# The first norm's result turned by 32x32 blocks on VectorE and by way of DRAM, with the expansion three slots later

## The chip, the cores and the metric

The kernel runs on one core of one Trainium2 chip, in one launch. The metric is the device time of that core in microseconds (us), as a median over runs. The engines are named PE (TensorE, matrix products and transposes through PSUM), DVE (VectorE), ACT (ScalarE), POOL (GpSimd) and SP (SyncE, which here only issues DMAs). PEld is the loading of weights into PE, which overlaps PE's products.

## The reference

One layer of a decoder with the norms behind the additions, in float32, for B = 16 sequences (called batches here) of T = 512 tokens with D = 256 features and 16 heads of 16:

```python
q = query @ wq + query @ Aq @ Bq * 4.0     # v likewise with Av, Bv; k = query @ wk
q, k = apply_rope(split(q)), apply_rope(split(k))
scores = where(causal, -1e9, q @ k.T / sqrt(16))
x = layernorm(x + softmax(scores) @ v @ wo)            # the first norm
h = butterfly(x @ W_exp + b_exp, up_weights, 1024)     # ten stages of 2x2 mixings
h = gelu(h + up_bias, approximate=False)
y = butterfly(h, down_weights, 1024) @ W_con + b_con + down_bias
out = layernorm(x + y)                                 # the second norm
```

## The kernel before

**Folded weights.** The ten butterfly stages are linear, so they are multiplied into the weights once: `wup` (256 x 1024) for the way up and `wdn` (1024 x 256) for the way down. This work is cut into tasks (`fold_tasks`) that a table `tasks_at` spreads over the first slots, up to slot 44. What is left of the second half for each batch is: `hidden` (the expansion: `ph` = `wup` times the turned x1, in 8 chunks of 128 units, L633), `gelus` (ACT), and `contract` (`py` = h times `wdn`, four token tiles t, each in two halves of four chunks, L660).

**Slots.** The order of all work is written out by hand: every engine runs its instructions in the order of the program. The program is a list of slots. A batch has four quads (two halves c of the heads, and an even and an odd head, par), each of five slots, so 20 slots (`per`). Slot s does `largest` for one block of scores of batch s/20 (PE L421, DVE L430 takes the row maxima) and `weights` for the same block of 15 slots before (PE L479 computes the scores again, with the row maximum taken off; ACT L493 takes the exponential, POOL L497 clears what lies above the diagonal). `weigh` (L521) multiplies the weights with v. A slot has a kind u = s mod 5; u = 0 and 1 work on 512 and u = 2 and 3 on 384 + 128 columns, u = 4 on 256 from both pairs. The two score tiles `pa` and `pb` have a single buffer each: the next slot's scores can be written when DVE and ACT have read these.

**Everything else** is hung onto slots: `add(s, f)` puts f behind the slot's scores and its `weigh`; `holes` come behind those. Within a slot the calls stand in the order in which they were added, batch by batch. For a batch that begins at slot s:

- `project_v` (pvv, L383) for the four token tiles, at s-3, s-1, s+4, s+14; `project` (pqk, L337, with a DVE copy L344 or L348, and the swap DMAs L351) for batch b+1 in the order of `chains`, all four in the hole of slot s+10; `turn` and `part` (POOL, ACT and a row of ones by DMA, L372) follow.
- `load_x` (the residual into z, L94) at s+9; `place_largest` (the maxima turned and written into a row of q by way of DRAM, L448 to L457) at s+11 and s+21.
- `normalize` (L553 reciprocal of the sums, L554 multiply), for c = 0 at s+27, 28, 29, 31 and for c = 1 at s+36, 37, 39, 40.
- `project_out` (L559; DVE adds the residual in L567 and takes statistics in L577 and L578) at s+41 and s+42, `spread`, `offset` and `centre` (L589 to L602, the first norm) at s+42, 43, 44.
- `turn_x1` at s+45: eight PE transposes (L616) into two of the three banks of `ps_w`, two DVE copies (L617) into `x1T`, and an addition of the biases to z on POOL (L621).
- `hidden` in pairs of chunks at s+46 to s+49 (DVE L644 or ACT L646 copy `ph` out, for chunks 0 and 4 and for the others), the eight `gelus` in the hole of s+50.
- `contract` halves at s+51, 52, 53, 55, 56, 58, 60, 63, each tile with the DVE chain L668, L577, L578; `spread` at s+63, `offset` at s+67, `centre` and `store` (L672) at s+68.

The last two batches have no later one to hide in; their second halves follow at the end with lists of their own. `largest` ends at slot 319, and the slots behind hold `weights` alone.

Of the kernel before, what the change touches and what calls it, by code (L numbers as in the profile page):

```python
# [11 lines left out]
F32 = mybir.dt.float32  # L12
BF16 = mybir.dt.bfloat16
AF = mybir.ActivationFunctionType
ALU = mybir.AluOpType
PSUM = bass.MemoryType.PSUM

P = 128
NH = 16
DH = 16  # L20
HG = 32
NG = P // HG
# [11 lines left out]
def decoder_layer(  # L34
# [18 lines left out]
    nc = tc.nc  # L53
    B, T, D = x.shape
    NT = T // P
    NC = D // P
    DHID = wcon.shape[0]
    NHC = DHID // P
# [5 lines left out]
    ring2 = ctx.enter_context(tc.tile_pool(name="ring2", bufs=2))  # L64
# [3 lines left out]
    dram = ctx.enter_context(tc.tile_pool(name="dram", bufs=4, space=bass.MemoryType.DRAM))  # L68
# [5 lines left out]
    def bank(name, shape):  # L74
        return ps_w.tile(shape, F32, tag="w", name=name)
# [10 lines left out]
    xTs, zs = {}, {}  # L86
# [24 lines left out]
    bias2 = const.tile([P, 2, D], F32, name="bias2")  # L111
# [197 lines left out]
    def fold_tasks():  # L309
        def up():  # L310
            yield from all_across(0, ya, DA)
            yield idle, lambda: nc.vector.tensor_add(
                hbias, ya[:, :, D : D + 1].rearrange("p c o -> p (c o)"), ubias
            )
            yield idle, lambda: nc.vector.tensor_add(
                bias2[:, 0, :], bias2[:, 0, :], bias2[:, 1, :]
            )

        def down():
            yield from all_across(1, wdn, D)  # L320
            yield from all_within(1, wdn, D)


        last = [
            (idle, lambda d=d, half=half: up_done(d, half))
            for d in range(NC)
            for half in range(2)
        ]
        return list(all_within(0, ya, DA)), mixed(down(), up()) + last
# [130 lines left out]
    state = {}  # L460
# [86 lines left out]
            nc.sync.dma_start(rows_of(sums, 1), rows_of(x, 0))  # L547
            nc.sync.dma_start(rows_of(even, 1), rows_of(x, 1))

    def normalize(b, c, t):  # L550
        x, sums = state["heads", b, c]
        ts = slice(t * P, (t + 1) * P)
        nc.vector.reciprocal(sums[:, ts], sums[:, ts])  # L553
        nc.vector.tensor_tensor(x[:, ts], x[:, ts], sums[:, ts], ALU.mult)  # L554

    def project_out(b, t):
        pw = bank(f"pwo_{b}_{t}", [P, D])
        for c in range(NC):
            nc.tensor.matmul(  # L559
                pw,  # L560
                state["heads", b, c][0][:, t * P : (t + 1) * P],
                wo_sb[:, c, :],
                start=(c == 0),
                stop=(c == NC - 1),
            )
        z = zs[b]
        nc.vector.tensor_add(z[:, t, :], pw, z[:, t, :])  # L567
        stats_of(1, b, t)
# [23 lines left out]
    def offset(which, b, t0=0, t1=NT):  # L592
        stats, norm = state["stats", which, b], state["norm", which, b]
        ts = slice(t0, t1)
        nc.vector.scalar_tensor_tensor(  # L595
            norm[:, 2, ts], stats[:, ts, 0], -1.0, norm[:, 1, ts], ALU.mult, ALU.mult
        )
# [10 lines left out]
            )  # L608


    def turn_x1(b, c):
        if c == 0:
            state["x1T", b] = ring2.tile([P, NC, T], F32, tag="x1T", name=f"x1T_{b}", bufs=1)
        pt = bank(f"pt1_{b}_{c}", [P, NT, P])
        for t in range(NT):
            nc.tensor.transpose(pt[:, t, :], zs[b][:, t, c * P : (c + 1) * P], ident)  # L616
        nc.vector.tensor_copy(  # L617
            state["x1T", b][:, c, :], pt.rearrange("p t q -> p (t q)")
        )
        if c == NC - 1:  # L620
            nc.gpsimd.tensor_tensor(  # L621
                zs[b],
                zs[b],
                bias2[:, 0:1, :].to_broadcast([P, NT, D]),
                ALU.add,
            )

    def hidden(b, hc, fused=False):
        if hc == 0:
            state["h", b] = hpool.tile([P, NHC, T], F32, tag="h", name=f"h_{b}")  # L630
        ph = bank(f"ph_{b}_{hc}", [P, T])
        for c in range(NC):
            nc.tensor.matmul(  # L633
                ph,
                wup[:, c, hc * P : (hc + 1) * P],
                state["x1T", b][:, c, :],
                start=(c == 0),
                stop=(c == NC - 1),
            )
        h = state["h", b][:, hc, :]  # L640
        if fused:
            nc.scalar.activation(h, ph, AF.Gelu, bias=hbias[:, hc : hc + 1])
        elif hc % 4 == 0:
            nc.vector.tensor_copy(h, ph)  # L644
        else:
            nc.scalar.copy(h, ph)  # L646

    def gelus(b, count=NHC):
        h = state["h", b]
        for hc in range(count):  # L650
            nc.scalar.activation(
                h[:, hc, :], h[:, hc, :], AF.Gelu, bias=hbias[:, hc : hc + 1]
            )
# [31 lines left out]
    per = PER_QUAD * NQ  # L685
    behind = PER_QUAD * BEHIND
# [3 lines left out]
    others = {s: [] for s in range(-head, last)}  # L690
    holes = {}
    chains = [(c, side) for c in range(NC) for side in range(2)]

    def add(s, f, *args):
        others[s].append(lambda: f(*args))

    def start_projection(b, side, c):
        state["pr", b, side, c] = project(b, side, c)
# [13 lines left out]
    for b in range(B):  # L712
        s = b * per
        if b > 0:

            at = {1: (-16, -11, -13, -9), B - 1: (-1, 4, 10, 10)}.get(b, (-3, -1, 4, 14))
            for t in range(NT):
                add(s + at[t], project_v, b, t)
        if b + 1 < B:

            add(s - head * (b == 0), load_xT, b + 1)
            at = {0: (2, 5, 7, 10), 1: (3, 6, 8, 11)}.get(b, (10, 10, 10, 10))
            for i, (c, side) in enumerate(chains):
                holes.setdefault(s + at[i], []).append(
                    lambda b=b, side=side, c=c: start_projection(b + 1, side, c)
                )
                turning = s + max(at[0] + 1 + 3 * i, at[i] + 1)
                for step in range(3):
                    add(turning + step, turn, b + 1, side, c, step)
                for step in range(1 + side):  # L730
                    add(turning + (6 if i == 3 else 4) + step, part, b + 1, side, c, step)
        add(s + 9, load_x, b)
        add(s + 11, place_largest, b, 0)
        add(s + 21, place_largest, b, 1)
        for c in range(NC if b + 1 < B else 1):
            for t in range(NT):
                at = (27, 28, 29, 31) if c == 0 else (36, 37, 39, 40)
                add(s + (at[t] if b + 1 < B else 29 + t), normalize, b, c, t)
        if b + 1 < B:
            for t in range(NT):  # L740
                add(s + 41 + t // 2, project_out, b, t)
            add(s + 42, spread, 1, b)
            add(s + 43, offset, 1, b)
            add(s + 44, centre, 1, b)
            for c in range(NC):
                add(s + 45 + (b + 2 == B), turn_x1, b, c)
        if b + 2 < B:

            late = 2 * (b + 3 == B)
            for hc in range(NHC - late):  # L750
                add(s + 46 + hc // 2, hidden, b, hc)
            holes.setdefault(s + 50, []).insert(0, lambda b=b, late=late: gelus(b, NHC - late))
            for hc in range(NHC - late, NHC):
                holes[s + 50].append(lambda b=b, hc=hc: hidden(b, hc, True))
            for t in range(NT):
                for half in range(2):
                    at = (11, 12, 13, 15, 16, 18, 20, 23)[2 * t + half]
                    if b + 3 == B and t == NT - 1:
                        at = (23, 25)[half]
                    add(s + 40 + at, contract, b, t, half)  # L760
            add(s + 63 + 2 * (b + 3 == B), spread, 2, b)
            add(s + 67, offset, 2, b)
            add(s + 68, centre, 2, b)
            add(s + 68, store, b)

# [2 lines left out]
    for hc, at in enumerate((7, 8, 9)):  # L770
        add(edge + at, hidden, y, hc)
# [8 lines left out]
    for t in range(NT):  # L780
        add(end + 2, normalize, z, NC - 1, t)
# [10 lines left out]
    for c in range(NC):  # L792
        add(end + 5, turn_x1, z, c)
# [13 lines left out]
    first, second = fold_tasks()  # L807
    fold = first + second
    tasks_at = dict(zip(range(2, behind), (0, 1, 2, 3, 4, 4, 5, 5, 5, 6, 9, 11, 14)))
    for s in range(behind, 2 * per + 5):  # L810
        tasks_at[s] = len(first) + -(-len(second) * (s - behind + 1) // (2 * per + 5 - behind))
    ahead = 0
    given = 0
    due = deque()
# [12 lines left out]
    for s in range(-head, last):  # L827
# [7 lines left out]
        if kinds and not (len(kinds) == 1 and kinds[0][2] % 2):  # L835
# [7 lines left out]
            elif u == PER_QUAD - 1:  # L843


                blocks = [(2, r, ps) for r, ps in enumerate((pair0, pair1))]
# [3 lines left out]
            else:  # L850
                for i, (fn, quad, _) in enumerate(kinds):
                    blocks = [(k, (r + i) % 2) for k, r in SLOTS[u]]
# [135 lines left out]
```

## Time and profile before

| | before |
|---|---|
| median of 3 runs | 1364.14 us (1358.62 to 1364.54) |
| the profiled execution | 1357.15 us |
| its span | 1355.4 us, granted PE clock 0.993 of full speed |
| PE busy | 1320.3 us (97%), 8728 instructions |
| DVE busy | 925.8 us (68%) |
| ACT busy | 707.3 us (52%) |
| POOL busy | 510.9 us (38%) |
| row maxima (L430, 384 columns) | 878 of 499 ns |
| expansion products (L633) | 512 of 604 ns, 235.8 us busy |
| contraction products (L660) | 1024 of 391 ns, 252.1 us busy |

The page of the profile gives the busy time of each engine, the chain of work that ended last with its shares by engine and line, and groups of instructions by line: busy us, mean ns of one, idle time before them and what ended it. Matmuls are pipelined: the length of a record is its latency, so what a row of them costs PE is read from the start of the first to the start of the next group in the timeline. Timeline rows give the start in us, the length, the engine, the line, what was written and read, shapes, and how many were joined in the row.

### The profile page before, as it was taken

The numbers are of one execution on the slowest core, as the hardware profiler recorded it, in microseconds if no ns is written. First come the engines' busy times: TensorE is split into PE (matmuls) and PEld (weight loads), VectorE is DVE, ScalarE is ACT, GpSimd is POOL, SyncE is SP. The second block draws the span as 40 slices with busy tenths as digits, with TensorE's granted clock in tenths as the row PEclk, the third lists the DMA queues.
The fourth block names the chain that finished last, engine by engine and source line by source line (L and its number), as shares of the span: only waits on it lengthen the run. The fifth ranks groups of instructions, "written<-read, shape, count | busy, mean of one in ns | idle before, by whom it ended". The sixth has DMA issues, their size and how long they took to land.

```text
span 1355.4 us, 23859 instructions
## 1 busy us (share of the span) xinstructions
PE 1320.3 (97%) x8728; PEld 702.5 (52%) x8728; DVE 925.8 (68%) x2949; ACT 707.3 (52%) x1079; POOL 510.9 (38%) x777
## 2 busy tenths in 40 slices
PE   8898999999999999999999999999999999998998
PEld 4453545455454545555454554545555454554555
DVE  4788757667685766758577685857768685776632
ACT  2575454454646445464645545464554546445643
POOL 3534215344251533425153352515335252531311
PEclk9998999999999999999999999999999999999999
DMA  5311010110102011010110101010110101000000
GB/s 172 120 45 45 22 59 30 40 45 30 68 30 74 30 41 45 30 67 30 67 35 31 57 30 68 30 60 30 40 60 30 68 30 55 30 27 32 30 12 31
DMA packets 45685, 63.49 MB, mean 47 GB/s; under 512 B 5752, under 2 KB 26232, under 8 KB 45568
## 3 DMA queue, kind: packets, MB, share of 16 engines
q1 hardware_dynamic: 41680, 56.42, 11.8%
q10 hardware_dynamic: 3888, 5.55, 1.3%
q8 instruction: 69, 1.13, 0.3%
q14 instruction: 48, 0.39, 0.1%
HBM read 23.40 MB, written 8.91 MB: 24 GB/s over the span
## 4 chain that ended last, share of the span: by engine, by line
PE 84%; DVE 11%; ACT 3%; issue 2%; DMA 0%; POOLq 0%; POOL 0%; DVEq 0%; SPq 0%; ACTq 0%
PE pb L479 19%; PE ph L633 17%; PE py L660 16%; PE po L521 10%; PE pqk L337 8%; DVE junk L430 5%; PE pvv L383 4%; PE pwo L559 3%; PE pa L421 3%; DVE bn L577 1%; PE pb L421 1%; PE pt L616 1%; ACT pT L493 1%; PE pa L479 1%; DVE z L567 1%
## 5 line engine op out<-in xcount | busy, mean ns | idle before, releaser
L430 DVE CUSTOM_DVE_ANT_0 junk<-pa,causal 128x384 bf16<-128x384 f32 (+2 forms) x878 | 438.3, 499 | 235.0 <-PE pa L421 176.1
L493 ACT ACTIVATE pT<-pb 128x1024 f32<-128x1024 f32 (+1 forms) x314 | 293.8, 936 | 377.3 <-PE pa L421 227.6
L497 POOL TENSOR_SCALAR_AFFINE_SELECT pT<-pT 128x256 f32<-128x256 f32 x512 | 202.5, 407 | 733.3 <-ACT pT L493 731.6
L479 PE MATMUL pb<-qz,kz 17*128 17x512 f32 (+2 forms) x1756 | 328.8, 473 | 16.1 <-ACT pT L493 12.1
L421 PE MATMUL pa<-kz,qz 32*128 32x384 f32 (+3 forms) x1756 | 329.2, 474 | 4.2 <-DVE mx L430 4.2
L660 PE MATMUL py<-wdn,h 128*128 128x256 f32 x1024 | 252.1, 391 | 0.0
L479 PEld LDWEIGHTS pb<-qz,kz 17*128 17x128 f32 (+1 forms) x1756 | 142.9, 183 | 179.5 <-issue 82.2
L633 PE MATMUL ph<-x1T,yb 128*128 128x512 f32 x512 | 235.8, 604 | 0.0
L660 PEld LDWEIGHTS py<-wdn,h 128*128 128x128 f32 x1024 | 185.1, 189 | 72.2 <-issue 36.2
L521 PE MATMUL po<-pT,vaug 128*32 128x512 f32 (+3 forms) x2048 | 179.5, 446 | 0.0
L633 PEld LDWEIGHTS ph<-x1T,yb 128*128 128x128 f32 x512 | 92.4, 189 | 122.3 <-issue 97.6
L421 PEld LDWEIGHTS pa<-kz,qz 32*128 32x128 f32 (+1 forms) x1756 | 143.7, 184 | 13.6 <-DVE mx L430 11.2
L553 DVE RECIPROCAL sums<-sums 128x128 f32<-128x128 f32 x128 | 121.1, 946 | 0.0
L337 PE MATMUL pqk<-xT,wqk 128*128 128x512 f32 x256 | 118.5, 613 | 0.0
L646 ACT COPY h<-ph 128x512 f32<-128x512 f32 x84 | 49.2, 585 | 123.2 <-PE ph L633 123.2
L521 PEld LDWEIGHTS po<-pT,vaug 128*32 128x32 f32 x2048 | 47.1, 109 | 102.3 <-issue 78.2
L430 DVE DVE_READ_ACCUMULATOR2_ANT mx<- 128x1 f32 x1024 | 84.5, 82 | 0.0
L337 PEld LDWEIGHTS pqk<-xT,wqk 128*128 128x128 f32 x256 | 48.0, 194 | 61.9 <-issue 57.4
L365 POOL TENSOR_TENSOR swap<-swap,rope_sb 128x512 f32<-128x512 f32 x62 | 79.6, 1283 | 0.0
L602 ACT ACTIVATE z<-z,norm 128x256 f32<-128x256 f32 x128 | 66.7, 589 | 24.6 <-DVE norm L595 24.5
L668 DVE TENSOR_TENSOR z<-py,z 128x256 f32<-128x256 f32 x64 | 27.1, 423 | 74.1 <-PE py L660 73.9
L430 DVE CUSTOM_DVE_ANT_0 junk<-pb,causal 128x256 bf16<-128x256 f32 (+3 forms) x146 | 63.6, 436 | 17.3 <-PE pa L421 4.0
(91 smaller groups left out, 1334.2 us busy)
## 6 DMA issues: line engine op xcount, KB each, us to landing
xT<-in_xT SPq DMA_DIRECT2D x16, 512.0 KB
swap<-qz SPq DMA_DIRECT2D x64, 128.0 KB
swap<-kz SPq DMA_DIRECT2D x64, 128.0 KB
z<-in_x SPq DMA_DIRECT2D x16, 512.0 KB
sums<-x SPq DMA_DIRECT2D x64, 128.0 KB
out_y<-z SPq DMA_DIRECT2D x15, 512.0 KB
x<-x SPq DMA_DIRECT2D x32, 128.0 KB
early<-in_wexpT ACTq DMA_DIRECT2D x1, 1028.0 KB
```

Of the source, the lines that this page charges most:

```text
L337: nc.tensor.matmul(pq, wqk[:, d, e : e + P], xTs[b][:, d, :], start=(d == 0), stop=(d == NC - 1))
L365: engine.tensor_tensor(swap, swap, rope_sb[:, 1, :], ALU.mult)
L421: lambda i=i, rows=rows, at=at, n=n, t=t, ps=ps: nc.tensor.matmul(ps[:, i, at : at + n], q[rows, par, t * P : n], k_[rows, par, 0:n], star ...
L430: lambda i=i, at=at, n=n, t=t, g=g, ps=ps: nc.vector.tensor_tensor_reduce(out=junk[:, 0:n], in0=ps[:, i, at : at + n], in1=causal[:, T - n ...
L479: lambda i=i, rows=rows, at=at, n=n, k=block, ps=ps: nc.tensor.matmul(ps[:, i, at : at + n], kt[rows, par, k * P : (k + 1) * P], qt[rows, ...
L493: nc.scalar.activation(pT[:, heads, 0:n], ps[:, :, at : at + n], AF.Exp)
L497: nc.gpsimd.affine_select(out=diag, in_=diag, pattern=[[0, 2], [1, P]], compare_op=ALU.is_ge, fill=0.0, base=0, channel_multiplier=-1,)
L521: nc.tensor.matmul(po[HG * g : HG * (g + 1), k * P : T], vaugs[b % 2][:, k, NG * c + g, first : first + HG], pT[:, g, at : at + n], start= ...
L553: nc.vector.reciprocal(sums[:, ts], sums[:, ts])
L602: nc.scalar.activation(zs[b][:, t, :], zs[b][:, t, :], AF.Identity, bias=norm[:, 2, t : t + 1], scale=norm[:, 1, t : t + 1],)
L633: nc.tensor.matmul(ph, wup[:, c, hc * P : (hc + 1) * P], state["x1T", b][:, c, :], start=(c == 0), stop=(c == NC - 1),)
L660: nc.tensor.matmul(py, state["h", b][:, hc, t * P : (t + 1) * P], wdn[:, hc, :], start=(hc == 0), stop=(hc == NHC - 1),)
```

## The change

For batches 0 to 13, the PE transposes and the two copies out of PSUM are replaced. DVE transposes each token tile of z in 32x32 blocks (four instructions of 128 x 256, SBUF to SBUF); four DMAs on SP, one for each band of 32 partitions, place the blocks in a DRAM tile, 128 KB each; and one DMA reads the tile back as `x1T` (512 KB), with tokens in blocked order. `hidden` reads it by a pattern with runs of 32. Batches 14 and 15 keep the transposes on PE. Around it the order of the slots is changed: the transposes stand ahead of slot s+45's other calls, the addition of the biases comes at s+47, the expansion begins at s+49 instead of s+46, with its last chunk fused with its gelu, and the contraction, the second norm and the store follow later. `project` is no longer all in one hole: one at s+7 and three at s+13. `project_v` moves by one to three slots, `load_x` by eleven, `normalize` is split into `invert` and `scale`, and the fold tasks are spread up to slot 47.

```diff
-    def normalize(b, c, t):
+    def invert(b, c, t):
+        sums = state["heads", b, c][1]
+        ts = slice(t * P, (t + 1) * P)
+        nc.vector.reciprocal(sums[:, ts], sums[:, ts])
+
+    def scale(b, c, t):
         x, sums = state["heads", b, c]
         ts = slice(t * P, (t + 1) * P)
-        nc.vector.reciprocal(sums[:, ts], sums[:, ts])
         nc.vector.tensor_tensor(x[:, ts], x[:, ts], sums[:, ts], ALU.mult)
...
+    def turn_x1_by_blocks(b):
+        blocks = ring2.tile([P, D // HG, NT, HG], F32, tag="blocks", name=f"blocks_{b}", bufs=1)
+        for t in range(NT):
+            nc.vector.transpose(blocks[:, :, t, :], zs[b][:, t, :])
+        turned = dram.tile([D // HG, HG, NG, P], F32, tag="turned", name=f"turned_{b}")
+        for n in range(NG):
+            nc.sync.dma_start(
+                turned[:, :, n, :].rearrange("f j k -> j f k"),
+                blocks[HG * n : HG * (n + 1)].rearrange("j f t i -> j f (t i)"),
+            )
+        x1T = ring2.tile([P, NC, T], F32, tag="x1T", name=f"x1T_{b}", bufs=1)
+        nc.sync.dma_start(x1T, turned.rearrange("(c f) j n k -> (f j) c (n k)", c=NC))
+        state["x1T", b] = x1T.rearrange("p c (n t i) -> p c t n i", t=NT, i=HG)
...
-                state["x1T", b][:, c, :],
+                state["x1T", b][:, c],
...
-            at = {1: (-16, -11, -13, -9), B - 1: (-1, 4, 10, 10)}.get(b, (-3, -1, 4, 14))
+            at = {1: (-16, -11, -13, -9), B - 1: (13, 13, 13, 13)}.get(b, (-3, 0, 5, 15))
...
-            at = {0: (2, 5, 7, 10), 1: (3, 6, 8, 11)}.get(b, (10, 10, 10, 10))
+            at = {0: (2, 5, 7, 10), 1: (3, 6, 8, 11)}.get(b, (7, 13, 13, 13))
...
-        add(s + 9, load_x, b)
+        add(s + 20, load_x, b)
...
-                at = (27, 28, 29, 31) if c == 0 else (36, 37, 39, 40)
-                add(s + (at[t] if b + 1 < B else 29 + t), normalize, b, c, t)
+                if b + 1 == B:
+                    add(s + 29 + t, normalize, b, c, t)
+                    continue
+                add(s + ((29, 30, 31, 32), (37, 38, 39, 40))[c][t], invert, b, c, t)
+                add(s + ((29, 30, 31, 32), (37, 38, 40, 41))[c][t], scale, b, c, t)
...
-            add(s + 43, offset, 1, b)
+            others[s + 43].insert(0, lambda b=b: offset(1, b))
             add(s + 44, centre, 1, b)
+        if b + 2 == B:
             for c in range(NC):
-                add(s + 45 + (b + 2 == B), turn_x1, b, c)
+                add(s + 46, turn_x1, b, c)
         if b + 2 < B:
-            late = 2 * (b + 3 == B)
-            for hc in range(NHC - late):
-                add(s + 46 + hc // 2, hidden, b, hc)
-            holes.setdefault(s + 50, []).insert(0, lambda b=b, late=late: gelus(b, NHC - late))
...
+            others[s + 45].insert(0, lambda b=b: turn_x1_by_blocks(b))
+            add(s + 47, add_biases, b)
+            for hc in range(NHC - 1):
+                add(s + 49 + (hc + 1) // 2, hidden, b, hc)
+            holes.setdefault(s + 53, []).insert(0, lambda b=b: gelus(b, NHC - 1))
+            holes[s + 53].append(lambda b=b: hidden(b, NHC - 1, True))
+            at = (14, 16, 18, 19, 23, 24, 26, 28)
+            if b + 3 == B:
+                at = (14, 16, 18, 19, 20, 23, 24, 25)
             for t in range(NT):
                 for half in range(2):
-                    at = (11, 12, 13, 15, 16, 18, 20, 23)[2 * t + half]
...
+                    add(s + 40 + at[2 * t + half], contract, b, t, half)
+            add(s + 40 + at[-1], spread, 2, b)
+            add(s + 70, offset, 2, b)
+            add(s + 71, centre, 2, b)
+            add(s + 72, store, b)
...
-    for s in range(behind, 2 * per + 5):
+    for s in range(behind, 2 * per + 8):
```

## The prediction

> **What bounds the kernel now.** I read three views in this order: busy time of each engine, then one batch of the steady part, then single slots of that batch. Page parts 1 and 4:
>
> ```profile
> PE 1320.3 (97%) x8728; PEld 702.5 (52%) x8728; DVE 925.8 (68%) x2949; ACT 707.3 (52%) x1079; POOL 510.9 (38%) x777
> PE 84%; DVE 11%; ACT 3%; issue 2%; DMA 0%; POOLq 0%; POOL 0%; DVEq 0%; SPq 0%; ACTq 0%
> ```
>
> PE is nearly always busy, but 11% of the chain that ends last is DVE. The busy times of stretches cut at the first transpose (L616) of successive batches show that the middle repeats:
>
> ```profile
> 645.40:725.10 79.70, 79.51 (x541) 42.10 (x540) 56.12 (x183) 42.64 (x63) 31.66 (x47) 1.00 0.13 45
> 725.10:804.80 79.70, 79.52 (x542) 42.09 (x541) 56.16 (x181) 42.63 (x63) 31.68 (x47) 1.00 0.13 45
> ```
>
> The columns are length, PE, PEld, DVE, ACT and POOL busy, granted clock, DMA share, GB/s. A batch takes 79.7 us and PE is busy in 79.5 of them, at a granted clock of 1.00. So any PE work that goes is time that goes, unless PE then waits. Whether it waits is seen in single slots. PE's timeline around 762 us (start, length, instruction):
>
> ```profile
> 762.39 0.59 PE L479 MATMUL pb<-qz,kz 32*128 32x384 f32 x2
> 763.47 1.99 PE L660 MATMUL py<-wdn,h 128*128 128x256 f32 x8
> 765.40 0.48 PE L479 MATMUL pb<-qz,kz 32*128 32x256 f32 x2
> 765.53 0.48 PE L421 MATMUL pa<-kz,qz 16*128 16x256 f32 x2
> ```
>
> and DVE's:
>
> ```profile
> 763.63 0.56 DVE L430 CUSTOM_DVE_ANT_0 junk<-pa,causal 128x384 bf16<-128x384 f32 x1
> ...
> 765.39 0.08 DVE L430 DVE_READ_ACCUMULATOR2_ANT mx<- 128x1 f32 x1
> 766.71 0.42 DVE L430 CUSTOM_DVE_ANT_0 junk<-pa,causal 128x256 bf16<-128x256 f32 x1 [1.24 <-PE pa L479]
> ```
>
> The slot starts at 762.39. DVE takes up its row maxima 1.24 us later and is done at 765.47; the next slot's scores (L421), which write the same PSUM, begin 0.06 us after that, 0.11 us later than they could. That gives the rule I use: **a slot lasts as long as its PE work, or until its row maxima end plus 0.06 us, whichever is longer.** Maxima take 1.42 us in slots of kind 0 and 1, 1.84 in kinds 2 and 3, 1.94 in kind 4 (slot number mod 5). Undisturbed they ask for 2.7, 3.1 and 3.2 us. If DVE is held by earlier work the maxima begin late, and the lateness falls on PE. At 795.89 two chains of L567, L577 and L578 held them until 797.34 instead of 797.13; they ended at 799.16, and the scores due at 798.91 came at 799.22: 0.31 us lost. Such losses add up to 1.3 us a batch before (slots 13 to 15, 18 to 20 and 23 to 25, counted from a batch's first).
>
> **What goes.** Per batch, for 14 of 16 batches, eight transposes and two copies. The groups of the two lines (busy us, mean ns, idle before):
>
> ```profile
> L616 PE MATMUL pt<-ident,z 128*128 128x128 f32 x128 | 17.6, 280 | 0.0
> L617 DVE COPY x1T<-pt 128x512 f32<-128x512 f32 x32 | 20.5, 683 | 0.0
> ```
>
> and PE's timeline at one batch's eight:
>
> ```profile
> 804.28 1.09 PE L616 MATMUL pt<-ident,z 128*128 128x128 f32 x8
> 805.30 0.70 PE L479 MATMUL pb<-qz,kz 17*128 17x512 f32 x2
> ```
>
> The 280 ns are latency; eight take 804.28 to 805.30 = 1.02 us of PE, and 14 x 1.02 = **14.3 us** go. Two copies of 0.683 us on DVE go as well.
>
> **What comes on DVE.** Four block transposes 128x256 f32, SBUF to SBUF, none in this trace. The nearest rows: batch statistics read the same 128x256 from SBUF in 0.428 us (L577); a 128x128 multiply takes 0.29 at least, 0.98 at most when it meets POOL (L554); a 128x128 reciprocal 0.947 (L553). Bounds 0.30 and 0.95, value 0.43, because L577 has the same size and place: 1.7 us for four. They stand ahead of the slot-45 work, wait for ACT's centre (L602), and in my count end about 1.6 us into slot 46, whose maxima then come late by 0.3: PE loses 0.07 us there. At 0.30 it loses nothing; at 0.62, 0.83; at 0.95, 2.15 us a batch.
>
> [...]
>
> **What comes on the queues.** SP gets four issues of 128 KB into DRAM, then a read of 512 KB that waits for them. A single issue takes 0.33 to 0.56 us on SP (rows 0.33, ones row 0.56), so four are 2 us; a small write (rows<-mT) to the read behind it takes 758.78 to 760.25 = 1.5 us; the 512 KB store to the load that waits for it takes 740.36 to 743.82 = 3.5 us. Chain about 2 + 2 + 3.5 = 7.5 us after the transposes end. The first expansion product now comes at slot 49, about 12 us after slot 46 starts, 10 after they end: hidden with some 2.5 us to spare. Behind the waiting read on SP stand the ones row (L372), the next swaps (L351) and the sums (L544); from their places they are due after the read can go. ACT and POOL get no new work. Cost 0. The DMA share in the steady part is 0.13, so bandwidth is free; bounds 0 and, at twice the chain, 15 us, 5 us a batch.
>
> L633 reads x1T in runs of 32 elements instead of 512. No row shows such a read by PE. Nearest is ACT's write of vaug in strides of two (L391: 256 elements in 0.39 us; 512 contiguous ones, L646, in 0.585), no dearer for it. The other bound: a product cut into four of 128 columns would go at the transposes' 0.127 each, 0.508 instead of 0.454 us (3.63 us for the eight of two chunks), 12% of 14.5 us a batch (4 x 3.63) = 1.7. Value 0.
>
> **What moves.** The PE work of a steady batch falls from 78.06 to 77.03 us. With the rule above, slot by slot, losses are 2.2 us instead of 1.3 (1.09 and 2.29 in my count). Two places make it:
> - Slot 59 (39 of the next batch) is of kind 4 and now ends with the second half of contract t=1. DVE, in program order, waits for that product, adds and takes statistics (0.42 + 0.43 + 0.18, about 1.05 with gaps), and then inverts t=2 of the next batch (0.95) ahead of the maxima of slot 60. These begin 2.1 us into it rather than 1.24, end at 3.56, and the slot holds only 2.67 us of PE work (scores, po and a pvv that moved in): **0.95 us lost a batch**. Before, slot 59 held only the pair L553/L554, and slot 60 had 3.57 us of PE work to cover it.
> - Slot 63: scale t=2, inverse and scale t=3 of c=1 now stand in slots 60 and 61, ahead of four L567 chains (1.05 each); the maxima of 63 begin 1.95 us into it instead of 1.24: 0.85 lost in 63, 0.45 before.
> The other edges are as before within 0.1. Of the projections three share one hole; the one that reuses a bank waits for a copy of 0.69 us while 1.77 us of another product runs. Cost 0.
>
> **Sum.** PE work -14.3. Steady losses 12 batches x (2.29 - 1.09) = +14.4, partly what I round to 1.0 from the trace's own 1.3 before: +11 to +14, I take 12. Start (slots 16 to 50): fold work spread to slot 47 with short slots between, losses 29.1 against 22.5 in the same count: +6.5, though before's real start has some 7 us more waits (on ACT) than I can count, so 0 to +6.5, I take 4. End: slots 300, 305, 307, 315 become too short (2.0 + 1.1 + 1.1 + 1.1), 303, 314, 319 no longer are (3.3): +1.9; two contract halves more (3.84 us) run beside waits of the last slots: -1.1. Sum -14.3 + 12 + 4 + 1.9 - 1.1 = **+2.5 us**. The profiled execution took 1357.15 us (1.75 around its span), 7 below the median 1364.14 of runs from 1358.62 to 1364.54. 1357 + 2.5 = 1360; from the median, 1367. I say 1363.
>
> **Rivals.**
> - *The losses are covered* (chance 0.27). If DVE's slack takes up the new chains, as it would if the slot-59 inverse ran before the add in time or ACT's side of the start shrinks, only PE's -14.3 and part of the end stays: 1345 to 1352. For it: PE 97% busy. Against: the 0.31 us at 798.9, from a smaller jam.
> - *The blocks are dear* (0.17). One mechanism: four transposes in slots 45 and 46 delay the maxima of 46. It decides from 0.43 us apiece; at 0.62 it gives 12 x 0.8 = +9 on top (1373), at 0.95 +25 (1388). For it: L554's 0.98 beside POOL, L553's 0.95. Against: L577.
> - *The new x1T is slow* (0.14): read in runs, 1.7 us x 14 = +24 (1387); or late from DRAM, +5 x 13 = +65 at twice the chain, and less from 10 us on. Nothing speaks for it but the absence of a row.
> - *Nothing to gain, transposes free already*: excluded by 804.28 to 805.30, PE dense on both sides.
>
> **Numbers.** Forecast 0.42, rivals 0.27, 0.17, 0.14. The measurement can't tell less than 0.5% (6.8 us: 1357.3 to 1371.0) from no change. Faster 0.27, same 0.42, slower 0.31. The forecast's own range is 1357 to 1370. The 8-in-10 range leaves out the lowest faster cases and the dearest slow ones: 1345 to 1386.
>
> **What would show it.** Right: steady batch 79.3 to 79.7 us; slot 60's scores of the next slot wait some 0.9 us for L430; transposes near 0.43 us; first L633 of a batch waiting for nothing. Wrong: a batch of 78.5 us or less (losses covered); transposes above 0.6 us with PE waiting at slot 46 to 47; L633 above 592 ns, or waiting for the read of x1T.

## The result, and the profile after

The changed kernel takes 1365.06 us (median of 20 runs, 1359.01 to 1370.56) against 1361.04 us for the kernel before (20 runs): a ratio of 1.0035 with a 95% interval of 1.0022 to 1.0049. That is slower by 0.35%: inside the predicted range and within the 0.5% that the prediction called "same", but clear of noise. The 1363 on record lay 1 us below the median of 1364.14 that was shown for before, so it forecast a slight gain, and the kernel became slightly slower. Run once more beside the experiments it gave 1.0042 (1.0026 to 1.0058). Two runs of all that follow (3682 us in the sixth experiment, 1407 us in the eighth) stood far apart from the others of their kernels and are left out of the medians.

The profiled execution after took 1363.26 us, with a span of 1361.5 us and a mean granted clock of 0.984 (0.993 before). Busy times, and the chain that ended last:

```profile
PE 1324.7 (97%) x8616; PEld 694.3 (51%) x8616; DVE 915.9 (67%) x2977; ACT 700.9 (51%) x1067; POOL 511.7 (38%) x777
PE 80%; DVE 14%; ACT 3%; issue 2%; DMA 0%; POOLq 0%; POOL 0%; DVEq 0%; ACTq 0%
```

112 transposes are gone and PE is still busy 97% of a longer span; in the chain PE's share fell from 84% to 80% and DVE's rose from 11% to 14%. Two steady batches of the changed kernel, cut at the first block transpose of each (columns as in the prediction):

```profile
567.96:647.47 79.51, 79.10 (x531) 41.18 (x530) 55.50 (x183) 41.90 (x62) 31.65 (x48) 1.00 0.19 58
647.47:726.98 79.51, 79.11 (x532) 41.13 (x530) 55.59 (x183) 41.96 (x62) 31.71 (x48) 1.00 0.19 58
```

A batch takes 79.5 us, as before. (Before it was 79.54, not 79.70: the prediction cut its stretches 0.16 us too long. The two rows of transposes at 724.74 and 804.28 give 79.54.) So **1.02 us of PE work a batch went and nothing was gained**. Where it went is seen at slots 59 to 61 (slot 59 starts at 542.78). DVE, then PE:

```profile
547.02 0.42 DVE L695 TENSOR_TENSOR z<-py,z 128x256 f32<-128x256 f32 x1 [0.96 <-PE py L687]
547.48 0.43 DVE L585 BATCH_NORM_STATS2 bn<-z 128x6 f32<-128x256 f32 x1
547.94 0.18 DVE L586 BATCH_NORM_AGGREGATE stats<-bn 128x2 f32<-128x6 f32 x1
548.04 0.92 DVE L553 RECIPROCAL sums<-sums 128x128 f32<-128x128 f32 x1
548.88 0.63 DVE L430 CUSTOM_DVE_ANT_0 junk<-pa,causal 128x512 bf16<-128x512 f32 x1
550.17 0.87 DVE L558 TENSOR_TENSOR x<-x,sums 128x128 f32<-128x128 f32 x1
```

```profile
546.91 0.70 PE L479 MATMUL pb<-qz,kz 32*128 32x512 f32 x2
548.55 1.13 PE L383 MATMUL pvv<-wv_sb,xT 128*128 128x256 f32 x4
549.62 1.13 PE L479 MATMUL pb<-qz,kz 32*128 32x512 f32 x4
550.30 1.13 PE L421 MATMUL pa<-kz,qz 16*128 16x512 f32 x4
```

DVE idles 0.96 us for the contraction, adds, takes statistics, inverts, and only then, 1.97 us into slot 60, begins the row maxima (L430). These end at 550.25; the scores of slot 61 (L421), which stand 0.02 us behind the slot's start when nothing holds them, come at 550.30 instead of 549.64: some 0.67 us lost. The loss doesn't look like a wait, because PE's records leave no gap in slot 61 up to the next product at 551.36:

```profile
549.62:551.36 1.74, 1.74 (x9) 0.59 (x8) 1.74 (x4) 1.01 (x3) 1.27 (x2) 1.00 0.23 75
```

The four score products of L479 run first and alone, and the four of L421 then take 550.30 to 551.36 = 1.06 us. Undisturbed, the two kinds run side by side and all eight take about that long (the first experiment shows it). So the share of busy time hides this loss, and a slot's length shows it. The blocks themselves, on DVE and then on SP:

```profile
567.96 1.42 DVE L644 STREAM_TRANSPOSE blocks<-z 128x256 f32<-128x256 f32 x4
569.31 0.69 DVE L430 CUSTOM_DVE_ANT_0 junk<-pa,causal 128x512 bf16<-128x512 f32 x1
```

```profile
569.41 2.05 SPq L647 DMA_DIRECT2D turned<-blocks  x4
573.62 0.38 SPq L652 DMA_DIRECT2D x1T<-turned  x1
```

Four transposes take 1.42 us in all, end 1.3 us into slot 46 (568.08), and its maxima begin at 569.31, on time. Issue and landing of the writes take 4.2 us; the read starts at 573.62 and the expansion at 580.26 waits for nothing.

By place, from the starts of slots in the timelines of the two profiled executions, the 6.1 us between the spans are (work that moved from one place to another included): up to slot 60 +0.8 us, slots 60 to 300 -0.2, slots 300 to 319 -0.1, from slot 319 to the end +5.6.

### The profile page after: what moved, and what is told of

It reads as the page before. It is cut to its first block, busy times and chain, and to the rows that moved or that the text cites. A ratio compares the mean times of both kernels' runs of the same rounds, so it can differ in the third digit from the quotient of the medians.

```text
span 1361.5 us, 23681 instructions
## 1 busy us (share of the span) xinstructions
PE 1324.7 (97%) x8616; PEld 694.3 (51%) x8616; DVE 915.9 (67%) x2977; ACT 700.9 (51%) x1067; POOL 511.7 (38%) x777
## 4 chain that ended last, share of the span: by engine, by line
PE 80%; DVE 14%; ACT 3%; issue 2%; DMA 0%; POOLq 0%; POOL 0%; DVEq 0%; ACTq 0%
PE pb L479 17%; PE ph L660 17%; PE py L687 16%; PE po L521 10%; PE pqk L337 8%; DVE junk L430 6%; PE pa L421 3%; PE pvv L383 3%; DVE bn L585 2%; DVE sums L553 2%; PE pb L421 1%; ACT pT L493 1%; DVE z L575 1%; PE pa L479 1%; PE pwo L567 1%
## 5 line engine op out<-in xcount | busy, mean ns | idle before, releaser
L430 DVE CUSTOM_DVE_ANT_0 junk<-pa,causal 128x384 bf16<-128x384 f32 (+2 forms) x878 | 436.2, 497 | 184.6 <-PE pa L421 143.1
L479 PE MATMUL pb<-qz,kz 17*128 17x512 f32 (+2 forms) x1756 | 333.3, 479 | 18.1 <-ACT pT L493 12.5
L421 PE MATMUL pa<-kz,qz 32*128 32x384 f32 (+3 forms) x1756 | 334.1, 480 | 4.6 <-DVE mx L430 4.6
L479 PEld LDWEIGHTS pb<-qz,kz 17*128 17x128 f32 (+1 forms) x1756 | 143.6, 185 | 189.2 <-issue 83.4
L660 PE MATMUL ph<-x1T,yb 128*128 128x512 f32 x512 | 239.6, 607 | 0.0
L421 PEld LDWEIGHTS pa<-kz,qz 32*128 32x128 f32 (+1 forms) x1756 | 144.5, 186 | 24.7 <-DVE mx L430 22.6
L660 PEld LDWEIGHTS ph<-x1T,yb 128*128 128x128 f32 x512 | 91.2, 189 | 121.6 <-issue 114.1
L337 PE MATMUL pqk<-xT,wqk 128*128 128x512 f32 x256 | 122.3, 620 | 0.0
L430 DVE CUSTOM_DVE_ANT_0 junk<-pb,causal 128x256 bf16<-128x256 f32 (+3 forms) x146 | 63.6, 436 | 33.4 <-ACT pT L493 17.5
L430 DVE DVE_READ_ACCUMULATOR2_ANT mx<- 128x1 f32 x1024 | 84.3, 82 | 0.0
L673 ACT COPY h<-ph 128x512 f32<-128x512 f32 x72 | 41.9, 581 | 75.5 <-PE ph L660 75.5
```

What stands on the lines that cost most here:

```text
L337: nc.tensor.matmul(pq, wqk[:, d, e : e + P], xTs[b][:, d, :], start=(d == 0), stop=(d == NC - 1))
L421: lambda i=i, rows=rows, at=at, n=n, t=t, ps=ps: nc.tensor.matmul(ps[:, i, at : at + n], q[rows, par, t * P : n], k_[rows, par, 0:n], star ...
L430: lambda i=i, at=at, n=n, t=t, g=g, ps=ps: nc.vector.tensor_tensor_reduce(out=junk[:, 0:n], in0=ps[:, i, at : at + n], in1=causal[:, T - n ...
L479: lambda i=i, rows=rows, at=at, n=n, k=block, ps=ps: nc.tensor.matmul(ps[:, i, at : at + n], kt[rows, par, k * P : (k + 1) * P], qt[rows, ...
L660: nc.tensor.matmul(ph, wup[:, c, hc * P : (hc + 1) * P], state["x1T", b][:, c], start=(c == 0), stop=(c == NC - 1),)
```

## The experiments

All are compared with the kernel before, run beside them on the same chip (medians 1359.9 us for the first four, 1358.8 for the fifth to eighth and 1360.2 for the others).

**1. The reciprocal first.** In slot 59:

```diff
-                add(s + ((29, 30, 31, 32), (37, 38, 39, 40))[c][t], invert, b, c, t)
+                at = s + ((29, 30, 31, 32), (37, 38, 39, 40))[c][t]
+                others[at].insert(0 if (c, t) == (1, 2) else len(others[at]), lambda b=b, c=c, t=t: invert(b, c, t))
```

> The changed kernel with one edit: in slot 59 the reciprocal of c=1, t=2 stands ahead of the addition of the contraction tile instead of behind it; nothing is left out. Theory (DVE's order gives the gain back): the row maxima of slot 60 then begin 1.2 to 1.3 us into the slot instead of 2.0, the scores of slot 61 wait no longer, and a steady batch falls from 79.50 to 78.6-78.8 us; over 13 to 14 batches 10 to 12 us less than the changed kernel, some 1353-1355 us beside a kernel before of 1361. Rival (what was lost lies in the start and at the end, and the DVE jam is covered by something else that would wait next): no more than 2 us gained.

Measured: 1348.97 us, ratio 0.992 (0.9893 to 0.9947), 16 us below the changed kernel, where 10 to 12 were expected. DVE at slots 59 and 60 (slot 60 starts at 542.39):

```profile
541.45 0.95 DVE L553 RECIPROCAL sums<-sums 128x128 f32<-128x128 f32 x1
542.50 0.42 DVE L695 TENSOR_TENSOR z<-py,z 128x256 f32<-128x256 f32 x1
542.96 0.43 DVE L585 BATCH_NORM_STATS2 bn<-z 128x6 f32<-128x256 f32 x1
543.42 0.18 DVE L586 BATCH_NORM_AGGREGATE stats<-bn 128x2 f32<-128x6 f32 x1
543.63 0.69 DVE L430 CUSTOM_DVE_ANT_0 junk<-pa,causal 128x512 bf16<-128x512 f32 x1
```

The reciprocal now fills the time in which DVE waited for the product, and the maxima begin 1.24 us into slot 60. In slot 61 the two kinds of score products start side by side again, and all eight are through at 546.17, 1.08 us after the first:

```profile
545.09 0.70 PE L479 MATMUL pb<-qz,kz 32*128 32x512 f32 x2
545.12 0.70 PE L421 MATMUL pa<-kz,qz 16*128 16x512 f32 x2
```

A steady batch takes 78.31 us:

```profile
558.31:636.62 78.31, 78.16 (x532) 40.73 (x531) 55.01 (x184) 41.96 (x63) 31.84 (x47) 1.00 0.19 59
```

Of the 1.2 us a batch, slot 61 gives 0.67 (3.78 to 3.11 us) and slot 64 gives 0.48 (4.94 to 4.46), where part of the lateness had been handed on to. So the loss of the steady part was this order, not the blocks.

**2. The transposes back on PE,** at the new places of all else:

```diff
-        if b + 2 == B:
+        if b + 1 < B:
             for c in range(NC):
-                add(s + 46, turn_x1, b, c)
+                add(s + 45 + (b + 2 == B), turn_x1, b, c)
...
-            others[s + 45].insert(0, lambda b=b: turn_x1_by_blocks(b))
-            add(s + 47, add_biases, b)
```

> The changed kernel with the transposes back on PE at slot s+45 (turn_x1 for all batches, no DRAM tile), all else at its new place; the same result. Theory (the blocks save 1.02 us of PE a batch and cost next to nothing themselves; the new order costs the rest): a steady batch of 80.4-80.5 us, 13 to 14 us more than the changed kernel, some 1378 us. Rival (the block transposes, their DMAs or the read of x1T in runs cost time of their own): less than 8 us more than the changed kernel.

Measured: 1375.61 us, ratio 1.0103 (1.0076 to 1.013), some 10 us above the changed kernel, between what theory (13 to 14) and rival (under 8) had named; the batch 80.32 us. So in the new order the blocks save 0.8 us a batch, 11 in all: slot 45 grew from 2.70 to 3.53 us only. There the eight transposes and the four products of pvv behind them take 1.89 us together (646.87 to 648.76), 0.82 more than the 1.07 of the products alone, where the transposes took 1.02 us in the kernel before. And the new order alone costs 80.32 - 79.54 = 0.8 us a batch. The two cancel.

**3. The fold as before.**

```diff
-    for s in range(behind, 2 * per + 8):
+    for s in range(behind, 2 * per + 5):
```

(and the same 5 in the divisor below it).

> The changed kernel with the fold tasks spread up to slot 44 as before instead of 47; the same result. Theory (the start loses by the granted clock and by waits, not by where the fold ends): within 2 us of the changed kernel, with the granted clock again 0.98-0.99 on the mean. Rival (the longer fold makes short slots 43 to 48 in which PE waits and its clock falls): 3 to 6 us less than the changed kernel and a mean clock nearer 0.99.

Measured: 1366.23 us, ratio 1.0048 (1.0032 to 1.0063), clock 0.9865 in the median. The longer fold is not what costs.

**4. The blocks alone,** in the kernel before, with the expansion left at s+46:

```diff
-            for c in range(NC):
-                add(s + 45 + (b + 2 == B), turn_x1, b, c)
+            if b + 2 < B:
+                others[s + 45].insert(0, lambda b=b: turn_x1_by_blocks(b))
+                add(s + 47, add_biases, b)
+            else:
+                for c in range(NC):
+                    add(s + 46, turn_x1, b, c)
```

> The kernel before with the block transposes and the way through DRAM in place of the transposes on PE, the biases added at s+47, and the expansion left at s+46; the same result. It prices the chain that the three slots hide. Theory: x1T is there 7.5 to 8 us after the transposes end, these end 1.3 us into slot 46, the expansion could begin 1.1 us into it, so PE waits 7.5 to 8.5 us in each of 13 to 14 batches: 90 to 110 us more than before. Rival (the read lands much sooner, the three slots were not needed): under 40 us more.

Measured: 1506.55 us (two runs), ratio 1.1071 (1.1031 to 1.111): 147 us more. The wait is the one foretold; PE's waits (us in all, times, longest):

```profile
PE ph L657 <- DMA x1T<-turned: 116.1, 14, 8.7
```

From the end of the transposes (712.8) to the first product (721.0) it is 8.2 us. What had not been foretold is the clock. Two-microsecond stretches (PE busy is the second number, the clock the third from the end):

```profile
712.00:714.00 2.00, 0.61 (x8) 0.00 (x0) 1.97 (x6) 1.02 (x1) 0.34 (x1) 0.83 0.35 128
718.00:720.00 2.00, 0.00 (x0) 0.00 (x0) 0.00 (x0) 0.00 (x0) 0.00 (x0) 0.50 0.81 181
722.00:724.00 2.00, 2.00 (x4) 0.94 (x3) 0.00 (x0) 0.00 (x0) 0.00 (x0) 0.50 0.00 0
726.00:728.00 2.00, 2.00 (x7) 0.65 (x9) 0.00 (x0) 0.31 (x1) 0.00 (x0) 0.76 0.00 0
```

Here PE works at half clock for 6 us after the wait is over (721.0 to 727.0), which costs about another 3 us, the half of it. The steady batches take 89.7 to 91.3 us, 90.4 on the mean. This, and that the runs' times went with their mean clocks, made the clock the next question.

**5. The order put further right:** on top of the first experiment,

```diff
-                add(s + ((29, 30, 31, 32), (37, 38, 40, 41))[c][t], scale, b, c, t)
+                add(at, scale, b, c, t)
...
-                add(s + 41 + t // 2, project_out, b, t)
-            add(s + 42, spread, 1, b)
-            others[s + 43].insert(0, lambda b=b: offset(1, b))
+                add(s + (41, 41, 42, 43)[t], project_out, b, t)
+            add(s + 43, spread, 1, b)
+            others[s + 44].insert(0, lambda b=b: offset(1, b))
```

> The changed kernel with the reciprocal of c=1, t=2 ahead of the contraction's addition as in the first experiment, the multiplications of t=2 and t=3 one slot earlier, and the output projection's last tile with its spread and offset one slot later, so that DVE's four chains stand in three slots; nothing is left out. Theory (DVE's order in slots 59 to 64 sets what is left of the waits): the steady batch falls from 78.3 us in the first experiment by 0.1 to 0.4 us, 1 to 5 us less in all, some 1345-1348. Rival (what is left are waits of slot edges that no order takes away): within 1 us of the first experiment.

Measured: 1346.18 us, ratio 0.9908 (0.9889 to 0.9928), the batch 78.13 us, 0.18 below the first experiment, in the low part of the 0.1 to 0.4 that were expected. It beats both kernels.

**6, 7 and 8. Idle products in three slots,** in the changed kernel, in the fifth experiment and in the kernel before:

```diff
+        if s in (32, 33, 34):
+            pf = bank(f"fill_{s}", [P, T])
+            for _ in range(2):
+                nc.tensor.matmul(pf, wo_sb[:, 0, 0:P], rope_sb[:, 0, :], start=True, stop=True)
```

> The changed kernel with idle work added: two products of 128x128 by 128x512 into a PSUM bank that nobody reads, behind the other work of each of slots 32, 33 and 34 (about 5.4 us of PE in all), where PE waits for DVE and ACT near 118 to 128 us and the granted clock then stands at 0.5 until 138 us. Theory (those waits lower the clock, and the lower clock costs the time by which the changed kernel is slower): the half-clock stretch from 121 to 138 us goes or shrinks, the mean clock rises by 0.003 to 0.006, and the kernel is 2 to 7 us faster than the changed one although PE does more. Rival (the clock follows something else, or costs nothing): the clock stays and the kernel is 0 to 5 us slower.

> The new order of the fifth experiment and the idle products of the sixth together; nothing is left out. If both theories hold the gains add: 2 to 7 us less than the fifth experiment, about 1340-1345. If the clock is not what the idle products move: 0 to 5 us more than the fifth.

> The kernel before with the same idle products in the same three slots, whose own trace has a half clock from 121 to 130 and 136 to 140 us. Theory (the clock's loss in the start has nothing to do with the change): 2 to 6 us less than before and a mean clock up by 0.003 to 0.005. Rival: 0 to 5 us more.

Measured: 1362.12 us, 1.0028 (1.0013 to 1.0042); 1341.91 us, 0.9885 (0.9865 to 0.9905); 1359.55 us, 1.0009 (0.9993 to 1.0024). The place where the clock fell did change. The changed kernel, then the same with idle products:

```profile
120.00:124.00 4.00, 3.06 (x24) 1.87 (x26) 3.86 (x14) 1.82 (x3) 1.69 (x4) 0.65 0.20 74
124.00:128.00 4.00, 3.57 (x28) 1.52 (x28) 3.79 (x10) 1.19 (x2) 2.35 (x4) 0.50 0.00 0
132.00:136.00 4.00, 4.00 (x16) 1.69 (x12) 2.52 (x6) 2.96 (x6) 0.85 (x2) 0.50 0.18 66
```

```profile
121.00:125.00 4.00, 3.66 (x30) 1.52 (x28) 3.79 (x12) 1.20 (x2) 2.00 (x4) 1.00 0.00 0
125.00:129.00 4.00, 3.52 (x27) 1.29 (x21) 3.71 (x7) 2.42 (x4) 3.70 (x3) 1.00 0.09 33
137.00:141.00 4.00, 3.66 (x29) 1.72 (x30) 3.29 (x13) 1.73 (x3) 0.81 (x2) 0.61 0.00 0
```

The half clock from 121 to 138 us is gone, but it comes back at 138 behind the next waits. Mean clocks rose (medians 0.9845 to 0.991; 0.985 to 0.992; 0.990 to 0.991), the times fell less: by the ratios to before about 1 us in the sixth, where 2 to 7 were expected, 4 in the seventh, as expected, and none in the eighth, where 2 to 6 were. In the sixth the idle products may have taken most of what the clock gave; no run here separates the two.

**9 and 10. Idle products in eleven slots** (17, 19, 25, 29, 32 to 34, 38, 39, 44, 49; one or two each), in the changed kernel and in the fifth experiment, and **the changed kernel again**:

> The changed kernel with idle products of the same kind in eleven slots of the start that end in a wait of PE (17, 19, 25, 29, 32 to 34, 38, 39, 44, 49; about 13 us of PE), nobody reads them. Theory (waits of about 1 us and more in the start are what drops the clock): hardly any half-clock stretch is left between 55 and 200 us, the mean clock is 0.993 or more, and the kernel is 2 to 6 us faster than the changed one in the same call, since most of the idle products stand where PE waits. Rival (the idle products only take the place of what the clock cost): the time of the changed kernel or up to 5 us more.

> The order of the fifth experiment with the idle products in eleven slots: the candidate for the best version. Theory: 0 to 4 us less than order and idle products in three slots (a ratio to before of 0.985 to 0.989). Rival: the additional idle products cost more than the clock gives, ratio 0.990 or more.

> The changed kernel itself once more, beside the others of this call on one chip, so that its clock and time and those of the kernel before are compared there. Theory (its steady part equals the kernel before, and what it loses it loses by the granted clock in the start): 3 to 5 us above before, the mean clock 0.002 to 0.004 lower, and at one clock the two agree within 1 us. Rival (the difference is waits, whatever the clock): at one clock still 3 us or more apart.

Measured: 1363.44 us, 1.0024 (1.0014 to 1.0034); 1345.43 us, 0.9885 (0.9867 to 0.9903); 1366.75 us, 1.0042 (1.0026 to 1.0058). By the ratios the ninth lies about 2.5 us below the changed kernel run beside it, inside the 2 to 6 expected, with a clock of 0.992 against 0.985; the tenth is no better than the seventh. These runs don't show how much the clock costs, since each mends it by adding work.

**11. The block transposes twice.**

```diff
-            nc.vector.transpose(blocks[:, :, t, :], zs[b][:, t, :])
+            for _ in range(2):
+                nc.vector.transpose(blocks[:, :, t, :], zs[b][:, t, :])
```

> The changed kernel with each of the four block transposes done twice over (same output). It tests the step on slot 46. Theory (the row maxima of slot 46 begin when the transposes end, and PE has 0.07 us or less to spare there): four take 1.42 us, eight 2.8 us; slot 46 lengthens by 1.1 to 1.3 us in each of 13 to 14 batches, 15 to 18 us more than the changed kernel. Rival (DVE's lateness is absorbed by the slots after): under 5 us more.

Measured: 1399.23 us, ratio 1.0277 (1.0252 to 1.0302): 32 us above the changed kernel, twice what was expected. Eight took 3.34 us rather than 2.8 (one of them 0.444 us in the median, where it was 0.403 in the changed kernel; why isn't shown), so the maxima of slot 46 were 1.9 us late, and a batch took 1.58 us more. PE's records leave 0.68 us of that idle. The rest is the clock again. After such a wait at 582 us:

```profile
583.00:584.00 1.00, 0.32 (x6) 0.07 (x4) 0.84 (x4) 0.00 (x0) 0.00 (x0) 1.00 0.50 97
585.00:586.00 1.00, 1.00 (x10) 0.15 (x8) 0.85 (x3) 0.99 (x1) 0.00 (x0) 0.56 0.98 250
586.00:587.00 1.00, 1.00 (x6) 0.21 (x2) 0.88 (x6) 0.03 (x1) 0.90 (x3) 0.50 0.01 2
588.00:589.00 1.00, 1.00 (x3) 0.34 (x2) 0.00 (x0) 0.00 (x0) 1.00 (x1) 0.73 0.75 184
```

Steady batches of this run take 82.76, 81.08, 82.73, 81.09, 82.73, 81.08, 82.74, 81.08 us: the same program, the same wait, and in every other batch 1.65 us on top, one stretch of some 3.4 us at half clock. The next takes 83.00 with another such stretch, and the three behind it take 81.08 to 81.10 with none. No PE work was changed here, so this is what a fallen clock costs.

## Why the prediction was right and wrong

**Right: the mechanism.** The rule of slots held: PE work or the end of the row maxima, whichever is later. The jam at slot 60 was foretold at 0.95 us and measured 0.67, that of slots 63 and 64 at 0.85 and measured 0.9; together the steady losses were to grow by 1.2 us a batch, of which the sum took 1.0, and grew by 1.0. The net over slots 60 to 300 was -0.2 us. Experiment 1 shows that this order is the cause: one reciprocal moved gives back 1.2 us a batch.

**Right: the blocks and their way.** Transposes at 0.43 us apiece: measured 0.403, or 1.42 for four, below the 0.62 and 0.95 apiece at which the rival was priced. Chain 7.5 us, hidden: 8.2 in the fourth experiment, hidden by the three slots. L660 reads x1T in runs at a median of 592 ns, the same as L633 before. No rival on these came in. That slot 46 has little to spare is borne out by the eleventh, where 1.9 us of lateness made it 1.58 longer.

**The rival "the losses are covered"** did not come in by itself, but one line of order brings it: 1349 us in the first experiment, inside its 1345 to 1352. The prediction even named the edit.

**Wrong: the last step of the sum.** The working came to +2.5 us. The figure put on record, 1363, was a middle between 1360 (from the profiled execution) and 1367 (from the median shown), and so lay 1 us below the median it would be compared with: a loss in the working became a small gain in the forecast. A difference must be carried to the time it is measured against: from 1361.04, the median of 20, the sum gives 1363.5 and the run gave 1365.1.

**Wrong: the terms of start and end.** The PE products of each place can be counted in the two traces and priced by their rows: 1.92 us for a contraction half, 1.02 for eight transposes, 1.07 for the four products of pvv. Up to slot 60, for example, two contraction halves, the transposes of one batch and four products of pvv are fewer. What a place takes beyond its change in work was lost there.

| place | PE work, us | time, us | lost, us | in the sum |
|---|---|---|---|---|
| up to slot 60 | -5.9 | +0.8 | 6.7 | 4 |
| slots 60 to 300 | -12.2 | -0.2 | 12.0 | 12 |
| slots 300 to 319 | -1.9 | -0.1 | 1.8 | 1.9 |
| from slot 319 on | +5.8 | +5.6 | -0.2 | -1.1 |

The work adds up to the -14.3 of the prediction, which was right, and so were the steady term and that of the short slots from 300 on. The step that failed in the working is the start (slots 16 to 50 in the prediction): its own count gave +6.5, and it took 4, because before's real start has waits that the count didn't find; 6.7 were lost. At the end three contraction halves more stand from slot 319 on (two behind it, and one in it), and in net the waits there hid 0.2 us of them instead of 1.1. These two make up the 3.6 us between +2.5 and the 6.1 of the profiled executions. That is one execution of each kernel; the medians differ by 4.0 us, and by 6.6 in the repeat.

What the start loses is priced as waits in the prediction. The two traces show another kind of cost as well: summing (1 - clock) over 2 us stretches, PE lost 8.5 us of clock before and 20.4 after; of the difference 5.1 lie before 70 us, 3.4 from 110 to 160, 1.7 from 160 to 240 and 1.7 near 1320. The first three make 10.2 us, more than the 6.7 lost there, so not all of it can have cost time. The prediction had read the clock only in the steady part, where it is 1.00.

How much of the difference the clock carries can't be settled to the microsecond. Over 63 runs of the kernel before the time falls by 1.07 us for each 0.001 of the mean clock, over 20 of the changed one by the same 1.07. The medians of the clock are 0.988 and 0.9845. At 0.986, lines fitted to the runs give 1362.6 us before and 1363.1 after, and for the repeat and the runs of before beside it 1364.9 and 1362.1. So 0.5 to 2.7 us of the 4.0 to 6.6 remain when the clock is the same: for the repeat neither the theory (within 1 us) nor its rival (3 or more). That is a regression, not an intervention; the eleventh experiment shows that the clock does cost, the idle products failed to win it back cleanly. Which wait of the start lowers it more often after the change (PE waits 2.51 us near 60 us where it waited 1.90 before) stays open.

## What to carry to other kernels

When work is taken off an engine that is always busy, look at the next engine's order in the slots that got shorter: here 14 us of TensorE went and one reciprocal, standing behind an addition that waited for a product, ate most of it; put ahead of that addition it filled the wait, and the kernel was 0.8% faster than before instead of 0.35% slower. In an order written by hand, an instruction that waits should stand behind those that could run meanwhile. Don't shrink a term that was counted on the ground of waits that can't be counted. And carry a predicted difference to the very time that it will be compared with.

## What was unexpected of the hardware

Here a wait cost PE more than its length. In the eleventh experiment a slot that was 1.58 us longer, 0.68 us of it idle in PE's records, was followed in every other of nine batches by some 3.4 us at a clock of 0.50, which cost another 1.65 us; an 8.4 us wait in the fourth was followed by 6 us at 0.50. The lost clock of the traces before and after comes in multiples of about 1.7 us (pieces of 1.7, 3.4, 5.1 and 8.5; a last one is cut short by the end of the span). The losses of 0.7 and 0.9 us in the steady part of the changed kernel, where PE's records leave 0.4 us of a batch idle (79.10 busy of 79.51), never lowered it. The falls of the eleventh experiment, at 257.4, 421.3, 585.1, 749.0 and 912.8 us, come 163.8 us apart, which is two of its batches (82.74 and 81.08). Which of two equal waits is followed by a fall, and why the last three were not, these runs don't explain.
